# A megakernel of attention, experts and state space: the order of work at the end of the first attention and around the expert gates

## The chip, the cores and the metric

The kernel runs on one NeuronCore of a Trainium2 chip. The metric is the device time of one launch in microseconds (us); the value before is the median of 3 runs. The engines are PE (TensorE: matmuls, with PEld its weight loads), DVE (VectorE), ACT (ScalarE), POOL (GpSimd) and SP (SyncE, which here issues DMAs). The profile is that of one further execution.

## The reference, cut to what matters

Four residual blocks act on `x` (4 batches x 512 rows x 256 channels); `ctx_768` is a context of 1601 rows x 192 channels for each batch. The change lies in the end of the first block and the start of the second and third.

```python
x = x + _L0_xattn_ref(_layernorm(x), ctx_768, ...)      # 16 heads of 16, 1601 keys
x = x + _L0_ffn_ref(_layernorm(x), Wg, W11, W12, W2)    # 8 experts, 2 for each row
x = x + _L1_xattn_ref(_layernorm(x), ctx_768, ...)      # top-32 attention, S4, FFN
x = x + _L1_ffn_ref(_layernorm(x), ...)                 # attention with switched heads

# first block
attn = einsum('bhqd,bhkd->bhqk', q, k) * scale
attn = softmax(clip(attn, -1e4, 1e4))
out = einsum('bhqk,bhkd->bqhd', attn, v) @ Wo + bo
# second block
topk_scores, topk_idx = top_k(softmax(x @ Wg), 2)       # the gates
fused = silu(x @ W11[e]) * (x @ W12[e]);  out = sum of topk_scores * (fused @ W2[e])
# third block
scores = (x @ Wq) . (ctx @ Wk);  only the 32 largest of 1601 are kept, then softmax
```

## The kernel before, in words

**The first attention** is `attend` (L81). Its 16 heads go in groups of four, so with 4 batches there are 16 groups (`gi`, 0 to 15). A head has 32 rows of a tile: 16 of data, one that carries the negated row maximum or the ones for the sum, the rest zero. Four heads of a group therefore stand in four row groups of the PE array and can be multiplied side by side. Per group there are two passes over the 1601 keys. The maxima (`maxima_mm`, L190, PSUM tiles `pss` of pool `ps_s`, three buffers) are scores of 128 queries by 512 keys, which DVE reduces to row maxima `mx`. The weights (`weights_mm`, L229, PSUM tiles `pst` of pool `ps_t`, three buffers) are scores the other way round, 128 keys by 512 queries with the maximum already subtracted, and ACT makes `pT` of them by Exp (L237). `gather` (L240) multiplies `pT` of a chunk of 128 keys with the values of the four heads into the one accumulator `acc`.

The order of PE is written out by hand (`tc.manual_schedule` for PE alone; the other engines are ordered by the framework). A step `t` is half a chunk: two heads of the weights and, 30 steps ahead (`LEAD`), two heads of the maxima of a later group, interleaved. A group has 13 chunks, so `NU` = 26 steps, and there are 416 steps, followed by 40 in which only what is left is emptied. In the last 30 steps there are no maxima left. The gather of a chunk stands four steps behind its weights. Further work (projections of coming groups, and what `at(t, ...)` orders for a later step) is a list of generators, `todo` and `due`, from which `step()` (L299) takes one piece in each odd step, and one more in each step behind the 416th.

When a group's last chunk is gathered, `taken` (L249) copies `acc` to `ou`, sends the sums of the softmax through a DMA (`sums`) to 128 partitions, takes reciprocals and sends them back by a second DMA (`r4`). Eleven steps later `scaled` (L259) spreads them by a matmul (`bc`, L265), and DVE multiplies (`oN`). When all four groups of a batch are there, `output` (L269) multiplies `oN` with `wo` for each of the four tiles of 128 queries (four matmuls each, tile `po` in pool `ps_p`, which has one buffer) and DVE adds the result to the residual `xr` (L277).

Behind the loop (L356 to L367) DVE and one matmul `pn` check that no score was clamped and that all sums are sound, and write `flag`. All engines load `flag` (L720) and branch on it (L721); with the data here the branch is not taken into `attend_any`.

**The second part** (from L734) holds the experts and the second attention. PE, DVE and ACT keep the order of the program there; POOL and SP are ordered by the framework. SP loads the weights of the second attention, the mask `tmask` and the context of batch 0 (`load_ctx2`, L793), and then the gate's weights `wg` (L1017). `run(keys2(0, 0))` (L1256) computes the keys of the second attention for the first two heads of batch 0 (L839, L840, four blocks of up to 512 keys, evicted by ACT, L843, then two mask rows by POOL, L846). Then, for each batch in turn (L1258 to L1267), DVE takes statistics of four tiles (`ln_stats`, L664 to L667, with a power by POOL, L669), normalises (L675), SP writes `xn` to DRAM (`xs`), PE transposes (L773), ACT copies (L774), and 16 small matmuls give the gates `pg` (L1266). The two PSUM buffers of keys and transposes are `mm0` and `mm1` (`bank`, L754). DVE then chooses two experts for each row (L1275 to L1303), PE counts rows by expert (`pc`, L1308), the keys of the other two heads follow on PE (`run(keys2(0, 1))`, L1310), and DVE and PE work out which rows go to which block of 128 (`pt`, L1379; `x_at`, L1383). POOL fetches experts' weights (`wb`) and rows (`xg`) by indirect DMAs (L1399), and PE begins the experts with transposing `xg` (L1422).

The lines that set when the last attention steps and the gates come:

```python
        ps_s = st.enter_context(tc.tile_pool(name="a_s", bufs=3, space=PSUM))
        ps_t = st.enter_context(tc.tile_pool(name="a_t", bufs=3, space=PSUM))
...
                x, y = weights_mm(gi, c, pair, pTs[gi, c]), s_unit(t + LEAD)
                for _ in range(2):
                    next(x), next(y, None)
```

Of the kernel before, what the change touches and what calls it, by code (L numbers as in the profile page):

```python
# [11 lines left out]
F32 = mybir.dt.float32  # L12
# [7 lines left out]
P = 128  # L20
# [60 lines left out]
def attend(nc, tc, a, xr, ident, ones, evac, normalized, flag):  # L81
# [10 lines left out]
    with ExitStack() as st:  # L92
# [135 lines left out]

        def weights_mm(gi, c, pair, pT):  # L229
            wd = P if c < NG - 1 else GL  # L230
            for j in (2 * pair, 2 * pair + 1):
                rows = slice(32 * j, 32 * j + 32)
                pst = ps_t.tile([P, S], F32, name="pst", tag="pst")
                nc.tensor.matmul(  # L234
                    pst[:wd, :], kTs[gi][rows, c * P : c * P + wd], qms[gi][rows, :], start=True, stop=True
                )
                nc.scalar.activation(pT[:wd, j, :], pst[:wd, :], AF.Exp)  # L237
                yield
# [30 lines left out]
        def output(b, qt):  # L269
            po = ps_p.tile([P, C], F32, name="po", tag="pj")  # L270
            for g in range(AG):
                nc.tensor.matmul(
                    po, oNs[b][:, g, qt * P : (qt + 1) * P], w["wo"][:, g, :], start=(g == 0), stop=(g == AG - 1)
                )
# [3 lines left out]
            yield  # L278

        def s_unit(s):  # L280
            gi, i = divmod(s, NU)
            return maxima_mm(gi, i // 2, 1 - i % 2) if gi < B * AG else iter(())
# [33 lines left out]
        for t in range(n_steps + 40):  # L316
# [6 lines left out]
            if gi < B * AG:  # L323
                if pair == 0:
                    pTs[gi, c] = p3.tile([P, 4, S], F32, name="pT", tag="pT")
                x, y = weights_mm(gi, c, pair, pTs[gi, c]), s_unit(t + LEAD)
                for _ in range(2):
                    next(x), next(y, None)
# [25 lines left out]

        m, low, one = [p3.tile([P, B * AG * 16], F32, name=n, tag="pT") for n in ("m", "low", "one")]
        nc.vector.tensor_reduce(m, mx.rearrange("p g q j n -> p (g q j) n"), AX.X, ALU.max)
        nc.vector.tensor_scalar(low, m, CLAMP, None, ALU.is_le)
        cnt = p1.tile([P, 2], F32, name="cnt")  # L360
        nc.vector.scalar_tensor_tensor(low, m, 104.0 - CLAMP, low, ALU.is_ge, ALU.mult, accum_out=cnt[:, 0:1])
        nc.vector.tensor_scalar(one, sums.rearrange("p g c -> p (g c)"), 0.5, None, ALU.is_ge)
        nc.vector.tensor_reduce(cnt[:, 1:2], one, AX.X, ALU.add)
        pn = ps_p.tile([P, 2], F32, name="pn", tag="pj")
        nc.tensor.matmul(pn, ones, cnt, start=True, stop=True)
        nc.vector.tensor_reduce(cnt[:, 0:1], pn, AX.X, ALU.add)
        nc.vector.tensor_scalar(flag, cnt[0:1, 0:1], 2.0 * P * B * AG * 16 - 0.5, None, ALU.is_lt)  # L367
# [255 lines left out]
def kernel(ctx: ExitStack, tc: tile.TileContext, a: dict, out: bass.AP):  # L623
# [114 lines left out]
    with ExitStack() as st:  # L738
# [37 lines left out]


# [13 lines left out]
        ts(tm4, tmask, 1.0 / XH, None, ALU.mult)  # L791
# [224 lines left out]
        wg = p_s.tile([P, 2, FE], F32, name="wg")  # L1016
        nc.sync.dma_start(wg, a["f_wg"].rearrange("(k p) e -> p k e", p=P))  # L1017
# [3 lines left out]
        nc.vector.tensor_copy(step, step_i)  # L1021
# [234 lines left out]
        run(keys2(0, 0))  # L1256
        pg = ps_b.tile([P, NT, FE], F32, name="pg", tag="po", bufs=1)
        for b in range(B):  # L1258
            xn = p_s.tile([P, QT, C], F32, name="xn", tag="s4", bufs=NSB)
            normalize([xn[:, i, :] for i in range(QT)], [xr[b * QT + i] for i in range(QT)])  # L1260
            nc.sync.dma_start(xs[b * S : (b + 1) * S, :].rearrange("(i p) c -> p i c", p=P), xn)
            xnT = p_s.tile([P, 2, S], F32, name="xnT", tag="s4", bufs=NSB)
            run(channels(xnT, [xn[:, i, :] for i in range(QT)]))
            for i in range(QT):
                for k in range(2):
                    nc.tensor.matmul(  # L1266
                        pg[:, b * QT + i, :], xnT[:, k, i * P : (i + 1) * P], wg[:, k, :], start=(k == 0), stop=(k == 1)  # L1267
                    )
        sm = p_s.tile([P, NT, FE], F32, name="sm")
# [8 lines left out]
        nc.scalar.activation(sm, sm, AF.Exp)  # L1278
        nc.vector.tensor_reduce(gm, sm, AX.X, ALU.add)
# [30 lines left out]
        run(keys2(0, 1))  # L1310
# [859 lines left out]
```

## Time and profile before

| | |
|---|---|
| median of 3 runs | 3650.86 us (3633.21 to 3656.53) |
| the profiled execution | 3655.28 us, its span 3653.5 us |
| mean granted clock of PE | 0.890 |
| busy: PE, DVE, ACT, POOL | 84%, 64%, 44%, 25% of the span |
| last maxima of the first attention | about 1031 us |
| last gather of the first attention ends | 1090.9 us |
| flag written | 1115.2 us |
| first instruction behind the branch | 1119.7 us |
| gates done, DVE begins to choose | 1165.5 us |
| `x_at` written | 1200.3 us |
| first matmul of the experts | 1203.6 us |

Times of day are from the span's start. Shares of busy time are averages over all stages; the stretch from 1031 to 1204 us is read from the timeline, where each line has start, length, engine, line of the program, operation and tiles, and in brackets the idle time before it and what ended it. An fp32 matmul is recorded as two passes, so `x8` is four matmuls.

### The profile page before, as it was taken

To read this page: it belongs to the slowest core of one execution; us is meant where nothing else is said; L and a number is where in the kernel's file an instruction comes from. 1 tells how busy PE (TensorE), PEld (TensorE's weight loads), DVE (VectorE), ACT (ScalarE), POOL (GpSimd) and SP (SyncE) were. 2 spreads that over 40 slices of the span, in tenths; PEclk is the share of its full clock that TensorE was granted. 3 is DMA by queue.
4 is the path that set the end of the run, shared out by engine and by line. 5 is a ranking of instruction groups with operands and counts; after the bars stand their busy time and mean duration, and the time that the engine had idled before them with its cause. 6 is when DMAs were issued, how large, how long until landed. Compare 5 with 4: busy or idle time off the path is not lost. (4 is left out here: it accounts for less than half of the span.)

```text
span 3653.5 us, 41683 instructions
## 1 busy us (share of the span) xinstructions
PE 3073.6 (84%) x16046; PEld 1704.0 (47%) x16046; DVE 2330.0 (64%) x3959; ACT 1619.5 (44%) x3326; POOL 930.9 (25%) x603
## 2 busy tenths in 40 slices
PE   6999999999986599789787977599865788887898
PEld 3433333333324599456555555466632334344354
DVE  3665565656623699598999899333326674766754
ACT  0254454445550377355555555122232344453454
POOL 1000000000001377410010100033317392763935
PEclk8699999999995699788898888799977798888899
DMA  2000000000001488300000000200010000000000
GB/s 68 1 15 1 1 15 1 1 1 1 1 1 51 132 291 281 117 28 14 1 14 1 1 1 1 96 1 0 1 38 0 0 1 5 2 2 5 1 6 6
DMA packets 48913, 110.03 MB, mean 30 GB/s; under 512 B 10450, under 2 KB 26139, under 8 KB 48700
## 3 DMA queue, kind: packets, MB, share of 16 engines
q0 software_dynamic: 20256, 70.66, 5.9%
q1 hardware_dynamic: 28444, 36.55, 3.2%
q8 instruction: 131, 2.15, 0.2%
q14 instruction: 82, 0.67, 0.1%
HBM read 97.62 MB, written 9.31 MB: 29 GB/s over the span
## 5 line engine op out<-in xcount | busy, mean ns | idle before, releaser
L203 DVE TENSOR_REDUCE mx<-pss 128x1 f32<-128x512 f32 x768 | 494.3, 685 | 294.2 <-PE pss L199 290.8
L237 ACT ACTIVATE pT<-pst 128x512 f32<-128x512 f32 (+1 forms) x832 | 452.5, 594 | 507.2 <-PE pss L199 318.8
L234 PE MATMUL pst<-qm,kT 32*128 32x512 f32 (+1 forms) x1664 | 507.0, 639 | 8.0 <-ACT pT L237 8.0
L199 PE MATMUL pss<-kT,qT 32*128 32x512 f32 x1536 | 485.7, 678 | 1.5 <-DVE mx L203 1.5
L981 PE MATMUL sum<-dg,e 128*128 128x128 f32 (+1 forms) x1664 | 267.6, 324 | 118.8 <-ACT dg L957 118.7
L1982 POOL TENSOR_TENSOR agg<-agg,tmp 128x1024 f32<-128x1024 f32 x112 | 263.3, 2378 | 336.0 <-DVE tmp L1981 335.8
L1933 ACT ACTIVATE pe<-pss,dnm 128x512 f32<-128x512 f32 x256 | 173.8, 683 | 337.8 <-DVE dnm L1931 337.6
L981 PEld LDWEIGHTS sum<-dg,e 128*128 128x128 f32 (+1 forms) x1664 | 239.2, 226 | 176.5 <-ACT dg L957 138.8
L1931 DVE TENSOR_REDUCE dnm<-pss 128x1 f32<-128x512 f32 x256 | 164.6, 684 | 196.3 <-PE pss L1928 195.9
L234 PEld LDWEIGHTS pst<-qm,kT 32*128 32x128 f32 (+1 forms) x1664 | 146.2, 180 | 294.6 <-ACT pT L237 270.7
L1873 POOL TENSOR_TENSOR dv<-dv,tmp 128x1024 f32<-128x1024 f32 x112 | 263.4, 2352 | 53.8 <-PE pss L1928 46.1
L1928 PE MATMUL pss<-dkT,dqT 64*128 64x512 f32 x512 | 182.9, 702 | 83.9 <-ACT pe L1933 83.2
L244 PE MATMUL acc<-pT,v 128*32 128x512 f32 (+1 forms) x1664 | 221.8, 604 | 0.0
L1872 DVE TENSOR_TENSOR tmp<-pp,mix 128x1024 f32<-128x1024 f32 x112 | 136.2, 1222 | 62.7 <-POOL dv L1873 49.1
L1431 PE MATMUL pa<-xgT,wb 128*128 128x128 f32 x1248 | 159.0, 282 | 19.6 <-ACT xgT L1424 19.5
L1399 POOL DMA_INDIRECT wb<-in_f_w,w_at x117 | 141.1, 1206 | 120.5 <-DVE t L1359 29.1
L199 PEld LDWEIGHTS pss<-kT,qT 32*128 32x128 f32 x1536 | 148.8, 193 | 36.2 <-DVE mx L203 24.8
L1431 PEld LDWEIGHTS pa<-xgT,wb 128*128 128x128 f32 x1248 | 154.0, 198 | 23.3 <-ACT xgT L1424 20.0
L1942 ACT COPY dpT<-tp 128x512 f32<-128x512 f32 x256 | 138.1, 595 | 53.9 <-PE tp L1940 53.5
L1940 PEld LDWEIGHTS tp<-ident,pe 128*128 128x128 f32 x1024 | 124.8, 148 | 60.7 <-issue 34.7
L931 DVE MAX8 tops<-ones 128x8 f32<-128x401 f32 x256 | 147.0, 574 | 6.7
L890 PE MATMUL pss<-xkT,xqT 64*128 64x512 f32 (+1 forms) x512 | 148.8, 610 | 2.7 <-ACT sc L897 1.3
(408 smaller groups left out, 5529.4 us busy)
## 6 DMA issues: line engine op xcount, KB each, us to landing
c<-in_ctxT SPq DMA_DIRECT2D x8, 800.5 KB
ys<-yo SPq DMA_DIRECT2D x39, 128.0 KB
c<-in_ctxT SPq DMA_DIRECT2D x8, 400.2 KB
xr<-in_x SPq DMA_DIRECT2D x16, 128.0 KB
xs<-xn SPq DMA_DIRECT2D x4, 512.0 KB
fwd<-in_dft SPq DMA_DIRECT2D x1, 2048.0 KB
inv<-in_idft SPq DMA_DIRECT2D x1, 2048.0 KB
out_dram<-ot SPq DMA_DIRECT2D x16, 128.0 KB
```

What stands on the lines that cost most here:

```text
L199: nc.tensor.matmul(pss[:, :wd], qTs[gi][rows, qt * P : (qt + 1) * P], kTs[gi][rows, o : o + wd], start=True, stop=True,)
L203: nc.vector.tensor_reduce(mx[:, gi, qt, j, n : n + 1], pss[:, :wd], AX.X, ALU.max)
L234: nc.tensor.matmul(pst[:wd, :], kTs[gi][rows, c * P : c * P + wd], qms[gi][rows, :], start=True, stop=True)
L237: nc.scalar.activation(pT[:wd, j, :], pst[:wd, :], AF.Exp)
L244: nc.tensor.matmul(acc[32 * j : 32 * j + 32, :], vs[b][:wd, c, AG * g + j, :], pT[:wd, j, :], start=(c == 0), stop=(c == NG - 1), tile_pos ...
L981: nc.tensor.matmul(pm[:w, c - 4 * n, :], e[:, c * P : c * P + w], dg, start=(h == 0 and c == 4 * n), stop=(h == 3 and c == cols[-1]),)
L1431: nc.tensor.matmul(pa[:, c, :], wbs[i, half][:, o : o + P], xTs[i][:, k, :], start=(k == 0), stop=(k == 1))
L1873: nc.gpsimd.tensor_tensor(v_t, v_t, tmp, ALU.add)
L1928: nc.tensor.matmul(pss[j], qT[rows, it * P : (it + 1) * P], kT[rows, :], start=True, stop=True)
L1931: nc.vector.tensor_reduce(nm, pss[j], AX.X, ALU.max, negate=True)
L1933: nc.scalar.activation(pe, pss[j], AF.Exp, bias=nm, accum_out=sums[u][:, it, j : j + 1])
L1982: nc.gpsimd.tensor_tensor(aggs[b][it], aggs[b][it], tmp2, ALU.add)
```

## The change

It has four pieces.

1. In steps without maxima (`lone`), all four heads' weights of a chunk are issued in the even step (`x` and a second generator `y` for the other two heads), and none in the odd step. Their PSUM tiles alternate between `ps_s`, which the maxima no longer use, and `ps_t`.
2. The outputs of the last batch are no longer one `output` for each query tile. `output_most` multiplies the first three groups 12 steps behind group 14's last gather, into two PSUM tiles `po2` of `ps_s` that stay open, each for two query tiles; `output_rest` adds the fourth group behind `scaled(15)`, and DVE adds to `xr`.
3. The check that writes `flag` becomes the generator `checked`, ordered 10 steps behind the last gather, ahead of `scaled(15)` in PE's order.
4. In the second part, `wg` is loaded first and kept in pool `p1`; the gates of the batches come ahead of any keys and are staggered: statistics of batch b, then normalising and transposing of batch b - 1, then the gate matmuls of batch b - 2. Converting `step`, `row`, `before`, `token` and `tm4` on DVE moves behind that loop. Of `keys2(0, 0)` one block is issued behind the gates' Exp; its other three blocks and `keys2(0, 1)` follow behind `pc`.

```diff
--- before.py
+++ after.py
@@ -226,11 +226,17 @@
             nc.vector.tensor_tensor(qms[gi], tp.rearrange("p a b -> p (a b)"), qTs[gi], ALU.add)
             yield
 
+        lone, last = [False], [0]
+
         def weights_mm(gi, c, pair, pT):
             wd = P if c < NG - 1 else GL
             for j in (2 * pair, 2 * pair + 1):
                 rows = slice(32 * j, 32 * j + 32)
-                pst = ps_t.tile([P, S], F32, name="pst", tag="pst")
+                last[0] ^= 1
+                if lone[0] and last[0]:
+                    pst = ps_s.tile([P, S], F32, name="pst", tag="pss")
+                else:
+                    pst = ps_t.tile([P, S], F32, name="pst", tag="pst")
                 nc.tensor.matmul(
                     pst[:wd, :], kTs[gi][rows, c * P : c * P + wd], qms[gi][rows, :], start=True, stop=True
                 )
@@ -275,6 +281,51 @@
                 if g == 1:
                     yield
             nc.vector.tensor_tensor(xr[b * QT + qt], po, xr[b * QT + qt], ALU.add)
+            yield
+
+
+        pos = []
+
+        def output_most(qt):
+            b = B - 1
+            if qt % 2 == 0:
+                pos.append(ps_s.tile([P, 2, C], F32, name="po2", tag="pss"))
+            for g in range(AG - 1):
+
+                nc.tensor.matmul(
+                    pos[-1][:, qt % 2, :], oNs[b][:, g, qt * P : (qt + 1) * P], w["wo"][:, g, :],
+                    start=(g == 0 and qt % 2 == 0), stop=False,
+                )
+                if g == 0:
+                    yield
+            yield
+
+        def output_rest(half):
+            b, g = B - 1, AG - 1
+            for i in range(2):
+                q = slice((2 * half + i) * P, (2 * half + i + 1) * P)
+                nc.tensor.matmul(
+                    pos[half][:, i, :], oNs[b][:, g, q], w["wo"][:, g, :], start=False, stop=(i == 1)
+                )
+            for i in range(2):
+                x = xr[b * QT + 2 * half + i]
+                nc.vector.tensor_tensor(x, pos[half][:, i, :], x, ALU.add)
+            yield
+
+        def checked():
+
+
...
+            pn = ps_p.tile([P, 2], F32, name="pn", tag="pj")
+            nc.tensor.matmul(pn, ones, cnt, start=True, stop=True)
+            nc.vector.tensor_reduce(cnt[:, 0:1], pn, AX.X, ALU.add)
+            nc.vector.tensor_scalar(flag, cnt[0:1, 0:1], 2.0 * P * B * AG * 16 - 0.5, None, ALU.is_lt)
             yield
 
         def s_unit(s):
@@ -324,8 +375,13 @@
                 if pair == 0:
                     pTs[gi, c] = p3.tile([P, 4, S], F32, name="pT", tag="pT")
                 x, y = weights_mm(gi, c, pair, pTs[gi, c]), s_unit(t + LEAD)
+                lone[0] = t + LEAD >= n_steps
+                if lone[0]:
+
+                    y = weights_mm(gi, c, 1, pTs[gi, c])
                 for _ in range(2):
-                    next(x), next(y, None)
+                    if not lone[0] or pair == 0:
+                        next(x), next(y, None)
             s = t + LEAD + 1
             if s % NU == 0 and s // NU <= B * AG:
                 done = s // NU - 1
@@ -340,8 +396,14 @@
                     gather(g2, i2 // 2, pTs.pop((g2, i2 // 2)))
                     if i2 // 2 == NG - 1:
                         taken(g2)
+                        if g2 + 1 == B * AG:
+                            at(t + 10, checked())
                         at(t + 11, scaled(g2))
-                        if g2 % AG == AG - 1:
+                        if g2 + 2 == B * AG:
+                            at(t + 12, (None for qt in range(QT) for _ in output_most(qt)))
+                        if g2 + 1 == B * AG:
+                            at(t + 14, (None for half in range(2) for _ in output_rest(half)))
+                        elif g2 % AG == AG - 1:
                             for qt in range(QT):
                                 at(t + 13 + 2 * qt, output(g2 // AG, qt))
             if pair == 1:
@@ -351,20 +413,6 @@
             if gi >= B * AG:
                 step()
         assert not todo and not late and not due and not now
-
-
-
...
-        nc.vector.tensor_scalar(flag, cnt[0:1, 0:1], 2.0 * P * B * AG * 16 - 0.5, None, ALU.is_lt)
 
 
 def attend_any(nc, tc, a, xr, ident, ones, evac, normalized, to_channels):
@@ -774,6 +822,8 @@
                 then(lambda k=k, tp=tp: nc.scalar.copy(dst[:, k, :], tp.rearrange("p a b -> p (a b)")))
                 yield
 
+        wg = p1.tile([P, 2, FE], F32, name="wg")
+        nc.sync.dma_start(wg, a["f_wg"].rearrange("(k p) e -> p k e", p=P))
 
         wq = p1.tile([P, 2, 2, P], F32, name="xwq")
         nc.sync.dma_start(wq, a["x_wq"].rearrange("(k p) (c m) -> p k c m", p=P, c=2))
@@ -788,7 +838,6 @@
         tmask = p1.tile([P, NT], U8, name="tmask")
         nc.sync.dma_start(tmask, a["tmask"])
         tm4 = p1.tile([P, NT], F32, name="tm4")
-        ts(tm4, tmask, 1.0 / XH, None, ALU.mult)
         cs, kTs, vs, qTs = {}, {}, {}, {}
 
         def load_ctx2(b):
@@ -1013,20 +1062,14 @@
         ys = dram.tile([NBK * P, C], F32, name="ys")
         NSB = 10
 
-        wg = p_s.tile([P, 2, FE], F32, name="wg")
-        nc.sync.dma_start(wg, a["f_wg"].rearrange("(k p) e -> p k e", p=P))
         step_i = p_s.tile([P, P], I32, name="step_i")
         nc.gpsimd.iota(step_i, pattern=[[1, P]], base=0, channel_multiplier=0)
         step = p_s.tile([P, P], F32, name="step")
-        nc.vector.tensor_copy(step, step_i)
         row_i = p_s.tile([P, 1], I32, name="row_i")
         nc.gpsimd.iota(row_i, pattern=[[0, 1]], base=0, channel_multiplier=1)
         row = p_s.tile([P, 1], F32, name="row")
-        nc.vector.tensor_copy(row, row_i)
         before = p_s.tile([P, P], F32, name="before")
-        ts(before, step, row, None, ALU.is_gt)
         token = p_s.tile([P, NT], F32, name="token")
-        ts(token, step[:, 0:NT], float(P), row, ALU.mult, ALU.add)
 
         u = da = ph = quarter = angle0 = fmax = fmin = None
 
@@ -1253,19 +1296,37 @@
 
 
         setup = s4_setup()
-        run(keys2(0, 0))
         pg = ps_b.tile([P, NT, FE], F32, name="pg", tag="po", bufs=1)
-        for b in range(B):
-            xn = p_s.tile([P, QT, C], F32, name="xn", tag="s4", bufs=NSB)
-            normalize([xn[:, i, :] for i in range(QT)], [xr[b * QT + i] for i in range(QT)])
+        xns, xnTs, mvs = {}, {}, {}
+
+        def normal(b):
+            xn = xns[b] = p_s.tile([P, QT, C], F32, name="xn", tag="s4", bufs=NSB)
+            mv, rs = mvs.pop(b)
+            for i in range(QT):
+                ts(xn[:, i, :], xr[b * QT + i], mv[:, i, 0:1], rs[:, i : i + 1], ALU.subtract, ALU.mult)
             nc.sync.dma_start(xs[b * S : (b + 1) * S, :].rearrange("(i p) c -> p i c", p=P), xn)
-            xnT = p_s.tile([P, 2, S], F32, name="xnT", tag="s4", bufs=NSB)
-            run(channels(xnT, [xn[:, i, :] for i in range(QT)]))
+
+        def gated(b):
             for i in range(QT):
                 for k in range(2):
                     nc.tensor.matmul(
-                        pg[:, b * QT + i, :], xnT[:, k, i * P : (i + 1) * P], wg[:, k, :], start=(k == 0), stop=(k == 1)
+                        pg[:, b * QT + i, :], xnTs[b][:, k, i * P : (i + 1) * P], wg[:, k, :], start=(k == 0), stop=(k == 1)
                     )
+
+        for b in range(B + 2):
+            if b < B:
+                mvs[b] = ln_stats([xr[b * QT + i] for i in range(QT)])
+            if 0 < b <= B:
+                normal(b - 1)
+                xnTs[b - 1] = p_s.tile([P, 2, S], F32, name="xnT", tag="s4", bufs=NSB)
+                run(channels(xnTs[b - 1], [xns[b - 1][:, i, :] for i in range(QT)]))
+            if b > 1:
+                gated(b - 2)
+        nc.vector.tensor_copy(step, step_i)
+        nc.vector.tensor_copy(row, row_i)
+        ts(before, step, row, None, ALU.is_gt)
+        ts(token, step[:, 0:NT], float(P), row, ALU.mult, ALU.add)
+        ts(tm4, tmask, 1.0 / XH, None, ALU.mult)
         sm = p_s.tile([P, NT, FE], F32, name="sm")
         gm = p_s.tile([P, NT], F32, name="gm")
 
@@ -1276,6 +1337,8 @@
         nc.vector.tensor_reduce(gm, sm, AX.X, ALU.max)
         tt(sm, sm, wide(gm), ALU.subtract)
         nc.scalar.activation(sm, sm, AF.Exp)
+        first_keys = keys2(0, 0)
+        next(first_keys)
         nc.vector.tensor_reduce(gm, sm, AX.X, ALU.add)
         nc.vector.reciprocal(gm, gm)
         tt(sm, sm, wide(gm), ALU.mult)
@@ -1307,7 +1370,7 @@
         flat = both.rearrange("p t e -> p (t e)")
         nc.tensor.matmul(pc[:, 0, :, :].rearrange("p t e -> p (t e)"), before, flat, start=True, stop=True)
         nc.tensor.matmul(pc[:, 1, :, :].rearrange("p t e -> p (t e)"), ones, flat, start=True, stop=True)
-        run(keys2(0, 1))
+        run(first_keys, keys2(0, 1))
         s0, s1 = [p_s.tile([P, NT, FE], F32, name=n) for n in ("s0", "s1")]
         nc.vector.tensor_copy(s0, pc[:, 1, :, :])
         place = p_s.tile([P, NT, FE], F32, name="place")
```

More of the change, by code (lines that the diff above doesn't have):

```diff
@@ L278, in output @@
             yield
+        pos = []
[23 more added lines that the diff above has]
+        def checked():
+            m, low, one = [p3.tile([P, B * AG * 16], F32, name=n, tag="pT") for n in ("m", "low", "one")]
+            nc.vector.tensor_reduce(m, mx.rearrange("p g q j n -> p (g q j) n"), AX.X, ALU.max)
+            nc.vector.tensor_scalar(low, m, CLAMP, None, ALU.is_le)
+            cnt = p1.tile([P, 2], F32, name="cnt")
+            nc.vector.scalar_tensor_tensor(low, m, 104.0 - CLAMP, low, ALU.is_ge, ALU.mult, accum_out=cnt[:, 0:1])
+            nc.vector.tensor_scalar(one, sums.rearrange("p g c -> p (g c)"), 0.5, None, ALU.is_ge)
+            nc.vector.tensor_reduce(cnt[:, 1:2], one, AX.X, ALU.add)
+            pn = ps_p.tile([P, 2], F32, name="pn", tag="pj")
[3 more added lines that the diff above has]
+            yield
         def s_unit(s):
@@ L353, in attend @@
         assert not todo and not late and not due and not now
[L357 to L367, printed above, removed]
 def attend_any(nc, tc, a, xr, ident, ones, evac, normalized, to_channels):
```

## The prediction

> **What bounds the kernel now.** I read the page's slices first, then the timeline of the stretch that the diff touches, then the waits of each engine in it, then windows for the granted clock. The chain of waits does not help: its pieces begin at 2317.80 us, behind the last branch, so the stretch must be read from the timeline.
>
> Slices of 91.3 us: busy tenths of PE and the granted clock.
> ```profile
> PE   6999999999986599789787977599865788887898
> PEclk8699999999995699788898888799977798888899
> ```
> The thirteenth slice (1096 to 1187 us) is the hole: PE busy six tenths at half clock. It holds the end of the first attention and the routing, which is what the diff edits.
>
> The last 15 chunks of the first attention, from about 1031 us, have no maxima beside them. One chunk (start, length, engine, line):
> ```profile
> 1074.04 1.12 PE L234 MATMUL pst<-qm,kT 32*128 32x512 f32 x2 [0.67 <-ACT pT L237]
> 1075.09 1.06 PE L244 MATMUL acc<-pT,v 128*32 128x512 f32 x8
> 1076.09 1.13 PE L234 MATMUL pst<-qm,kT 32*128 32x512 f32 x6
> 1077.24 1.57 ACT L237 ACTIVATE pT<-pst 128x512 f32<-128x512 f32 x3 [1.45 <-PE pst L234]
> 1077.89 1.12 PE L234 MATMUL pst<-qm,kT 32*128 32x512 f32 x2 [0.67 <-ACT pT L237]
> ```
> Each fp32 matmul is two passes, so x6 is three heads, side by side in 1.13 us, because a head uses 32 rows of the array. There are three pst buffers. The fourth head waits 0.67 us for ACT and then runs alone for 1.05. A chunk takes 3.85 us (1074.04 to 1077.89). Four at once is seen in the main loop, where pst and pss share the row groups:
> ```profile
> 1002.00 0.69 PE L234 MATMUL pst<-qm,kT 32*128 32x512 f32 x1
> 1002.01 0.69 PE L199 MATMUL pss<-kT,qT 32*128 32x512 f32 x1
> 1002.02 0.69 PE L234 MATMUL pst<-qm,kT 32*128 32x512 f32 x1
> 1002.02 0.69 PE L199 MATMUL pss<-kT,qT 32*128 32x512 f32 x1
> 1003.16 1.57 ACT L237 ACTIVATE pT<-pst 128x512 f32<-128x512 f32 x3 [1.59 <-PE pss L199]
> ```
> The tail, in order, and the branch that reads the flag:
> ```profile
> 1096.10 2.04 PE L265 MATMUL bc<-r,spread 4*128 4x512 f32 x2 [5.22 <-DMA r<-rs]
> 1098.99 3.78 PE L272 MATMUL po<-wo,oN 128*128 128x256 f32 x8 [0.85 <-DVE oN L266]
> 1115.01 0.14 DVE L367 TENSOR_SCALAR flag<-cnt 1x1 int32<-1x1 f32 x1
> 1119.70 0.23 POOL L1019 IOTA step_i<- 128x128 int32 x1 [485.88 <-DVEq L721]
> ```
> The engines' branch behind the flag, from the view of its line (length in ns, start):
> ```profile
> L721 PEldq COMPARE_BRANCH  x1: 3448/3448/3448, 1115.8 to 1115.8; - x1
> ```
> The sums go through DMA twice (PE idle 5.2 us, and its clock falls), four output tiles follow, then the flag, then PE's branch of 3.45 us; all engines leave together near 1119.7. Then the second part:
> ```profile
> 1125.61 0.17 DVE L791 TENSOR_SCALAR tm<-tmask 128x16 f32<-128x16 uint8 x1 [10.46 <-DMA mrow<-in_vmask]
> 1129.52 2.05 PE L839 MATMUL pk<-c,xwk 128*128 128x512 f32 x2 [14.74 <-DMA c<-in_ctxT]
> 1165.49 0.29 DVE L1275 COPY sm<-pg 128x128 f32<-128x128 f32 x1 [11.78 <-PE pg L1266]
> 1176.78 1.13 PE L839 MATMUL pk<-c,xwk 128*128 128x512 f32 x2
> ```
> The same in a window (busy time of PE, PEld, DVE, ACT, POOL; then granted clock, DMA share, GB/s):
> ```profile
> 1130.00:1166.00 36.00, 34.48 (x112) 23.80 (x110) 12.48 (x45) 6.66 (x12) 6.08 (x5) 0.50 0.17 59
> ```
> DVE stands behind tmask, and PE behind the context (14.7 us) for keys that nothing needs yet; the gates come behind both, and PE runs all of it at clock 0.50, a 128x512 matmul in 2.05 us a pair of passes against 1.13 at 1176.78.
>
> **The change, part by part** (positive is saved).
>
> *A, chunks of four heads.* Removed per chunk: the wait of 0.67 and the lone head's 1.05. Left on PE: four heads at once, 1.05 from start to the gather's start (1077.89 to 1078.94), and the gather, 1.00 to the next heads (1075.09 to 1076.09): 2.05. ACT needs 4 x 0.485 = 1.94 (three take 1.57, one 0.60, so one more costs 0.485), so PE and ACT are nearly even. The fourth head's second buffer use frees when ACT has done two heads of the chunk before: 1.16 + 0.60 + 0.485 + 0.05 = 2.30 after that chunk's start; the period settles between, at 2.175. From the gather at 1032.80 to that at 1086.60 there are 14 periods, 53.8 us; they become 14 x 2.175 = 30.5. Added: 0.5 at the start, where buffers of the last maxima are still read (1031.19 to 1032.13); 0.65 for the transposes of the last row maxima, 1.05 for group 14's bc, 0.6 for the copy of acc, all of which hid in the old waits; seven of the twelve early output matmuls, 0.5 each (1111.88: four in 1.99 us), less 0.6 taken up by the slack: 2.9; and 1.6 in the last chunk, because the second po2 leaves only one ps_s buffer. So 30.5 + 7.3 = 37.8, a gain of 16.0. Behind it come five more output matmuls and the last gathers: 1.0 + 1.0 + 1.05 + 0.5 + 1.0 + 1.1 = 5.65, where 1086.60 to 1090.88 is 4.28: 1.4 lost. A = 14.6. Bounds: 0 (a period of 3.4) and 20 (2.05, outputs free); I take the one near the main loop's four at once.
>
> *B, tail.* From acc's end E (1090.88) the two DMAs, bc and oN stay: oN at E + 8.05. The first three groups' output matmuls are gone from here; four matmuls are left at half clock, 0.95 each (3.78 for four): E + 11.9; the last two additions (0.42 each, 0.45 apart) end at E + 12.85. The check's DVE work (1.22, 0.29, 0.42, 0.23, 0.42) and its matmul fit into the DMA waits, being covered by the 5.2 us; if that cover were gone it would cost about 1 us, for pn stands ahead of bc on PE. The flag is written at about E + 4.3. PE's load of the flag (0.49) and its branch (3.45) can then run while DVE still adds: E + 8.2 + 0.4 + 0.49 + 3.45 = E + 12.5, with DVE's own load last, E + 13.5. Before, it was 1119.70 - 1090.88 = 28.8. B = 15.3. Bounds: 12.7 (the branch waits for the last matmul, E + 11.9 + 4.2) and 17 (full clock: bc 1.13, oN at E + 7.15, the branch at E + 11.6).
>
> *C, gates first.* From the common start X: DVE needs no DMA. Statistics of a batch take 2.42 (1126.36 to 1128.78), POOL's power is covered by the next batch's statistics, normalising takes 1.38: the second batch is normal at X + 10.1. Then PE is unbroken: rest of its transposes to X + 11.1, four gates of 3.6 (16 matmuls, 1150.17 to 1154.03 less a wait of 0.26) and two more transpositions of 1.75: X + 29.0. ACT's copies (0.59 x 2) hide, as gates run two batches behind. The old time is 1165.45 - 1119.70 = 45.75. C = 16.7. wg's DMA, moved past nine on SP's queue, is issued in 0.41 and is not waited for; it puts the context 0.45 later, and no one waits for that now. Converting step, row, tmask (1.1 us of DVE) now hides behind PE's gates. Bounds: 14 (DVE and PE not overlapped so well) and 24 (clock rises, rival 2).
>
> *D, keys behind the routing.* One block runs on PE during the 6.9 us in which DVE chooses experts: free. The other three stand ahead of the second half's four, behind pc. From pc's start (1172.39) the old keys end at +9.4 and PE then waits until +13.1 for rows. New: in full-clock time 2.1 + 2.1 + 0.87 + 7.2 = 12.3; if the clock rises after 3.4 us, as at 1176.78, they end at +15; wholly at half clock, at +23.5. With the first, pt begins 1.9 late, but its matmuls run in half of 7.05, and x_at is no later than rows of the second half allow, about +25 against +27.9. POOL takes that back: the mask rows (3.1 to 3.4 us a pair) of the first half now fall among the six weight fetches (1.28 each), which end about +25, and xg queues behind their bytes. D = 0. Bounds: -10 (pt starts at +23.5 and takes 7.05 twice: +37.6) and +4.
>
> **Sum.** 14.6 + 15.3 + 16.7 + 0 = 46.6. The profiled execution took 3655.3 (span 3653.5): 3608.7. It is 4.4 over the median of the three runs, so on the median's scale 3604.
>
> **Rivals.**
> 1. *Keys become the bound* (D at its bad end): the row for it is 1129.52 to 1142, keys at half clock for 13 us. Then 3604 + 10 = 3614. Against it: the keys behind pc did speed up.
> 2. *The clock rises in the gates.* For it: outputs sped up at about 1111 us after 12 us of work. Against: the window 1130 to 1166 stays at 0.50 with PE busy 34.5 of 36. Then PE's 18 us behind X + 11 take about 11: 3597. The Trainium skill (TensorE: Matmul & The Clock Gate, Part 1) says the clock is raised after one busy window, about 3.4 us; by that rule this rival would be the forecast. The trace of before disagrees in that window. By the rule the sum is 3597, by the row 3604.
> 3. *The chunks only come down to 2.9 to 3.3 us*, for want of free buffers or because PE cannot pass from four row groups to the gather without draining. The additions then partly hide, some 5 us of them left: A = 53.8 - 14 x period - 5 - 1.4, 1 to 7, and 3612 to 3617. Against it: the main loop makes the same passage from eight heads to the gather with no idle time of its own.
> 4. *Given back in the experts*: weights, not xg, start them. Half of C goes and D is at its bad end: 3604 + 8 + 10 = 3622.
> 5. *Slower: heads one by one.* If the three ps_s buffers came free only in turn with ACT, each head would take 1.13 + 0.62, a chunk 7.0 + 1.0 = 8.0 and A = 14.6 - 14 x (8.0 - 2.175) = -67; B and C give 32, and the time is 3651 + 35 = 3686. It decides from a chunk of 2.175 + 46.6/14 = 5.5 us on. Against it: with six buffers two heads at least are free at once.
>
> **How the numbers follow.** Forecast 0.46, rival 1 0.14, rival 2 0.15, rival 3 0.14, rival 4 0.06, rival 5 0.05. About 1%, 36.5 us, is what a measurement here can tell from no change, so the border is 3614. Faster: 0.43 + 0.15 and half of rivals 1 and 3, 0.14: 0.72. Slower: 0.02, the rest 0.26. The range takes rival 2 with the runs' own spread (17 under the median) below, and rivals 1, 3 and 4 above: 3580 to 3626. The likeliest alone: 3594 to 3614.
>
> **What would show it.** A: gathers 2.2 us apart from 1035 us on and ACT's 1.45 us idle gone. B: the first POOL iota about 13.5 us behind acc's last gather, with the flag written before bc. C: no PE wait for the context, sm's copy 29 us behind that iota. D: xg's first transpose near +31 behind pc. The prediction is wrong if the gathers stay over 3 us apart, if the branch begins only behind the last addition, or if pt waits for the keys by more than 5 us.

## The result, and the profile after

| | before | after |
|---|---|---|
| median of 20 runs (us) | 3655.31 | 3625.27 |
| lowest to highest | 3633.21 to 3687.92 | 3610.92 to 3638.82 |
| profiled execution; its span | 3655.28; 3653.5 | 3634.1; 3632.2 |

The ratio is 0.9918, with an interval of 0.9899 to 0.9938: 30.0 us saved (22.7 to 36.9), or 0.8%. 3625 lies inside the range by 0.7 us, at its upper edge, and outside the likeliest case's own.

For the readings below, the stretch is cut at six marks: M, the last row maximum; E, acc's end (the start of its copy); X, the first instruction behind the branch; S, the copy of the gates; pc, the places' matmul; XG, the first transpose of the experts' rows.

| stage (us) | before | after | saved | forecast |
|---|---|---|---|---|
| M to E (A) | 58.75 | 43.96 | 14.8 | 14.6 |
| E to X (B) | 28.78 | 15.87 | 12.9 | 15.3 |
| X to S (C) | 45.79 | 27.88 | 17.9 | 16.7 |
| S to pc | 6.90 | 6.89 | 0 | 0 |
| pc to XG (D) | 31.23 | 41.58 | -10.4 | 0 |
| M to XG | 171.45 | 136.18 | 35.3 | 46.6 |

The 35.3 lies inside the interval of the medians. The two profiled executions differ by less, 21.3: after's stood 4.7 us later already at M (1036.89 against 1032.17), ahead of all changed code, and lost 9.3 behind XG. Most of the 9.3 is in the last stage, whose code is the same, where one execution ran a stretch at half clock and the other did not. The same pair of matmuls, first after, then before, from the timeline of PE:
```profile
2686.44 3.78 PE L1951 MATMUL pk<-dxT,d_wk 128*128 128x512 f32 x4 [0.69 <-ACT dqT L1947]
```
```profile
2713.29 1.98 PE L1888 MATMUL pk<-dxT,d_wk 128*128 128x512 f32 x4 [0.69 <-ACT dqT L1884]
```
It need not all be chance. From XG to the end the changed kernel took 2459.1 here and 2459.0 when profiled again (e8, below), against 2449.9 before and 2453.9 and 2452.3 in e1 and e2, which keep the old second part; and the medians save 30.0 where the stages up to XG save 35.3. On the other hand e5, which has the gates first too, took 2453.9. Whether the change costs some 5 us there, or only the clock does, no run settles.

After, the slices (90.8 us each):
```profile
PE   6999999999997699688887877699764787887898
PEclk6799999999995899888989888899867798888899
```
The thirteenth slice (1090 to 1180 us) still holds the hole: PE is busy seven tenths there instead of six, at a clock of still five tenths.

*A.* The timeline of the lone chunks: start, length, engine, line, then what the engine had waited for.
```profile
1048.20 1.14 PE L240 MATMUL pst<-qm,kT 32*128 32x512 f32 x8
1049.27 1.07 PE L250 MATMUL acc<-pT,v 128*32 128x512 f32 x8
1049.42 4.07 ACT L243 ACTIVATE pT<-pst 128x512 f32<-128x512 f32 x8 [0.29 <-PE pst L240]
1050.27 1.41 PE L240 MATMUL pst<-qm,kT 32*128 32x512 f32 x8
1051.61 1.07 PE L250 MATMUL acc<-pT,v 128*32 128x512 f32 x8
...
1061.65 1.06 PE L250 MATMUL acc<-pT,v 128*32 128x512 f32 x8
1062.64 1.13 PE L295 MATMUL po<-wo,oN 128*128 128x256 f32 x4
1063.70 1.14 PE L240 MATMUL pst<-qm,kT 32*128 32x512 f32 x8
```
Heads are x8, four of two passes, in 1.14; gathers with nothing else between them start by turns about 2.07 and 2.33 apart (2.34 in the pair above), 2.2 in the mean, where 2.175 was forecast. ACT's idle time ahead of a group is 0.29, where it was 1.45. Two output matmuls (x4) stand between two chunks and cost their full 1.06.

*B.* The same view, at the tail's end, and the branch by line (length in ns, start):
```profile
1085.11 0.14 DVE L328 TENSOR_SCALAR flag<-cnt 1x1 int32<-1x1 f32 x1
...
1088.90 3.78 PE L307 MATMUL po<-wo,oN 128*128 128x256 f32 x8 [0.85 <-DVE oN L272]
1092.72 0.76 DVE L312 TENSOR_TENSOR xr<-po,xr 128x256 f32<-128x256 f32 x2 [0.95 <-PE po L307]
1096.65 0.43 DVE L712 BATCH_NORM_STATS2 ln_st<-xr 128x6 f32<-128x256 f32 x1 [3.17 <-DVEq L769]
1096.72 0.23 POOL L1066 IOTA step_i<- 128x128 int32 x1 [459.82 <-DVEq L769]
```
```profile
L769 PEldq COMPARE_BRANCH  x1: 3522/3522/3522, 1089.5 to 1089.5; - x1
L769 PEldq EVENT_SEMAPHORE  x1: 51/51/51, 1093.1 to 1093.1; - x1
L769 DVEq COMPARE_BRANCH  x1: 72/72/72, 1093.4 to 1093.4; - x1
L769 DVEq EVENT_SEMAPHORE  x1: 21/21/21, 1096.5 to 1096.5; - x1
```
PE is behind its branch at 1093.1, beside the additions, as forecast. DVE branches only behind its last addition, and 3.1 us pass until its event: its record of 72 ns does not show them, the gap to the event does. The profile of before has such a gap of 3.7 us, in the view of which the prediction showed PE's line alone:
```profile
L721 DVEq COMPARE_BRANCH  x1: 72/72/72, 1115.8 to 1115.8; - x1
L721 DVEq EVENT_SEMAPHORE  x1: 21/21/21, 1119.5 to 1119.5; - x1
```

*C and D.* Windows of after: busy PE, PEld, DVE, ACT, POOL; granted clock, DMA share, GB/s. First X to S, then pc to the routing's pt, then pt to x_at.
```profile
1096.72:1124.60 27.88, 21.11 (x97) 20.04 (x98) 14.76 (x58) 4.68 (x8) 5.68 (x14) 0.50 0.54 168
1131.49:1155.96 24.47, 23.67 (x33) 7.89 (x33) 20.11 (x59) 3.14 (x6) 7.73 (x5) 0.50 0.19 64
1155.96:1169.87 13.91, 13.87 (x65) 13.72 (x64) 0.00 (x1) 0.21 (x1) 4.97 (x4) 0.50 0.27 77
```
The two last, before:
```profile
1172.39:1185.50 13.11, 9.40 (x20) 3.60 (x20) 10.84 (x47) 1.98 (x4) 1.22 (x1) 0.76 0.12 40
1185.50:1200.33 14.83, 14.10 (x64) 13.81 (x64) 8.62 (x14) 0.00 (x0) 8.79 (x7) 0.50 0.58 176
```
From pc to pt it takes 24.47 us at clock 0.50, with PE busy 23.67 of them; the seven blocks of keys fill 22.5 of that (1133.48 to 1155.96). The rows for pt's first half are written early enough: DVE begins them at pc + 11.84, as before. So pt, once it starts, runs without a break, but 11.4 us later than before (24.47 against 13.11):
```profile
1143.33 5.00 DVE L1437 TENSOR_TENSOR rows<-step,slot 128x1024 f32<-128x1024 f32 x2
1151.73 2.35 DVE L1437 TENSOR_TENSOR rows<-step,slot 128x1024 f32<-128x1024 f32 x2
1155.96 13.87 PE L1442 MATMUL pt<-ids,rows 128*128 128x39 f32 x64
1169.87 0.20 DVE L1446 CAST x_at<-pt 128x39 int32<-128x39 f32 x1 [15.79 <-PE pt L1442]
```

### The profile page after: what moved, and what is told of

It reads as the page before. It is cut to its first block, busy times and chain, and to the rows that moved or that the text cites. A ratio compares the mean times of both kernels' runs of the same rounds, so it can differ in the third digit from the quotient of the medians.

```text
span 3632.2 us, 41689 instructions
## 1 busy us (share of the span) xinstructions
PE 3063.2 (84%) x16046; PEld 1699.6 (47%) x16046; DVE 2330.0 (64%) x3959; ACT 1615.9 (44%) x3326; POOL 930.9 (26%) x603
## 5 line engine op out<-in xcount | busy, mean ns | idle before, releaser
L240 PE MATMUL pst<-qm,kT 32*128 32x512 f32 (+1 forms) x1664 | 494.9, 642 | 0.7 <-ACT pT L243 0.7
L199 PEld LDWEIGHTS pss<-kT,qT 32*128 32x128 f32 x1536 | 149.3, 194 | 35.8 <-DVE mx L203 24.8
L1494 PEld LDWEIGHTS pa<-xgT,wb 128*128 128x128 f32 x1248 | 152.8, 197 | 24.5 <-ACT xgT L1487 20.5
L1991 PEld LDWEIGHTS pss<-dkT,dqT 64*128 64x128 f32 x512 | 56.3, 201 | 202.0 <-ACT pe L1996 146.6
```

Source lines behind the costliest of these rows:

```text
L199: nc.tensor.matmul(pss[:, :wd], qTs[gi][rows, qt * P : (qt + 1) * P], kTs[gi][rows, o : o + wd], start=True, stop=True,)
L240: nc.tensor.matmul(pst[:wd, :], kTs[gi][rows, c * P : c * P + wd], qms[gi][rows, :], start=True, stop=True)
L1494: nc.tensor.matmul(pa[:, c, :], wbs[i, half][:, o : o + P], xTs[i][:, k, :], start=(k == 0), stop=(k == 1))
L1991: nc.tensor.matmul(pss[j], qT[rows, it * P : (it + 1) * P], kT[rows, :], start=True, stop=True)
```

## The experiments

Three questions: what each part does alone, what D's loss hangs on, and what B's last 2.4 us are. Ratios are to runs of the kernel before on the same chip.

**e1_lone: the chunks of four heads alone** (before with piece 1 of the change; shown is where the heads are issued).
```diff
+                lone[0] = t + LEAD >= n_steps
+                if lone[0]:
+                    y = weights_mm(gi, c, 1, pTs[gi, c])
                 for _ in range(2):
-                    next(x), next(y, None)
+                    if not lone[0] or pair == 0:
+                        next(x), next(y, None)
```


> Before plus piece 1 alone (four heads at a time). Theory (the parts add up as the stage times of the two traces say): gathers 2.2 us apart; from the gather two steps ahead of the first lone chunk to the end of acc 61.9 us before, about 41 here, because nothing but the last row maxima, one bc and the copy of acc is added; tail and gates as before. Gain about 20 us, ratio 0.9945. Rival (the early outputs are what fills PE, and the chunks by themselves are bound by ACT and its buffers near 3 us): gain 9 to 12.

Measured: 0.9928 (0.9893 to 0.9963). M to E and pc to pt:
```profile
1041.55:1077.50 35.95, 35.58 (x258) 9.63 (x254) 3.57 (x7) 31.18 (x62) 0.00 (x0) 1.00 0.01 1
1155.55:1169.63 14.08, 14.08 (x20) 4.82 (x20) 11.81 (x47) 1.76 (x3) 1.22 (x1) 0.50 0.11 37
```
PE is busy 35.58 of 35.95: chunks alone save 22.8 of 58.75, more than the 20.5 forecast, and the tail behind E is 3.5 shorter (25.29) without an edit there: three of its four output tiles ran at the higher clock (2.0 us instead of 3.78), where before only one did. So of the change's 43.96, 8.0 are the early outputs. The second line is unexpected: with the old order of keys, four blocks behind pc run at 0.50, where before's profile has 0.76. In e2 they do so too.

**e2_tail: the outputs and the check moved, heads as before, second part as before** (shown against after; the lines of piece 4 are taken back too).
```diff
-                lone[0] = t + LEAD >= n_steps
+                lone[0] = False
```


> Before plus pieces 2 and 3 alone (early outputs, flag ahead of bc), chunks of two and two as before. Theory: the twelve early matmuls (6 us) go mostly into PE's waits of 0.67 us a chunk and of the emptying steps, so acc ends 0 to 3 us later, and from there to the first instruction behind the branch it takes 16.0 instead of 28.8: gain 10 to 13 us, ratio 0.997. Rival (PE works in order, so the waits for ACT stay as they are and the matmuls come on top): acc ends 6 us later, gain 7.

Measured: 0.9952 (0.9918 to 0.9986). E to X is 15.59, so the tail's gain (13.2) needs no other part. M to E grew by 7.6, but the clock fell in that window:
```profile
1030.16:1096.51 66.35, 61.60 (x284) 17.05 (x282) 3.80 (x8) 33.18 (x63) 0.00 (x0) 0.92 0.00 1
```
e3 shows 4.5 of growth there at the same clock with unchanged code, so about 3.1 belong to the outputs. That the rest of them hides in the old chunks' waits for ACT is argued from these lengths, not tried alone. In the new chunks they do not hide: outputs and last chunk cost 8.0, where the prediction's price was 5.9.

**e3_gates: gates first and keys behind the routing, the first attention as before** (piece 4 whole; shown are its lines on the keys).
```diff
-        run(keys2(0, 0))
...
+        first_keys = keys2(0, 0)
+        next(first_keys)
...
-        run(keys2(0, 1))
+        run(first_keys, keys2(0, 1))
```


> Before plus piece 4 alone (gates ahead of the keys). Theory: from the first instruction behind the branch to the copy of the gates 27.9 us instead of 45.8 (saves 17.9), and seven blocks of keys at half clock ahead of pt cost 10.4: gain 7.5 us, ratio 0.998. If the clock rises in the keys, about 16 to 20. Rival (the cost behind pc came from the early fetches of the shortened tail, not from the keys): pt is not late here and the gain is 17.

Measured: 1.0002 (0.9973 to 1.0031). X to S is 27.88, 17.9 saved; pc to XG is 41.60, 10.4 lost. The rest, 7.5 us or 0.2%, is too small to be seen in the time. Windows of M to E, of a piece of it, and of pc to pt:
```profile
1036.24:1099.51 63.27, 55.26 (x260) 13.03 (x258) 3.80 (x8) 33.18 (x63) 0.00 (x0) 0.92 0.00 1
1050.00:1064.00 14.00, 11.98 (x44) 2.77 (x40) 0.25 (x1) 6.22 (x12) 0.00 (x0) 0.69 0.01 1
1163.14:1187.60 24.46, 23.66 (x32) 7.88 (x32) 20.11 (x59) 3.15 (x6) 7.73 (x5) 0.50 0.20 64
```
The code of the first two is before's: 0.69 for 14 us is a dip of the clock, and the window is 4.5 us longer than before's. The third repeats after's 24.47 to 0.01 us.

The parts by stages, M to XG: e1 24.8, e2 4.8, e3 3.0; e2 and e3 without their dips 9.3 and 7.5. Their 41.6 exceed the whole's 35.3 because the outputs lose their cover (8.0 less 3.1, 4.9) and the 3.5 that e1's tail gained from the clock cannot be gained beside e2's; against that, e1 and e2 paid some 1.5 each for the half clock behind pc, which is in D already. That makes 36.2; 0.7 of what is left is e2's gain from X to S.

**e8_changed_again: the changed kernel once more.**

> The changed kernel as it is, beside the others on one chip. Theory: the same stages as in its first profile (44.0 us from the last row maximum to the copy of acc, 15.9 to the first instruction behind the branch, 27.9 to the copy of the gates, 38.4 from pc to x_at), ratio to before 0.990 to 0.993; what differs elsewhere, some 5 us at a time, is the clock. Rival (the keys' half clock behind pc was chance in the first profile): pt starts 13 to 15 us behind pc.

Measured: 0.989 (0.9849 to 0.9931). All stages up to XG repeat within 0.2 us (M to E 43.95, pc to XG 41.54) and so does the clock behind pc:
```profile
1134.52:1158.99 24.47, 23.67 (x32) 7.89 (x33) 20.12 (x59) 3.15 (x6) 7.75 (x5) 0.50 0.19 64
```

**e4_keys_late: the seven blocks behind the experts.**
```diff
-        run(first_keys, keys2(0, 1))
...
         run(powers)
+        run(first_keys, keys2(0, 1))
```


> The changed kernel, with all keys of batch 0 but the first block moved behind the experts, into the stretch of 32 us in which PE waits for the experts' rows. Theory: pt waits for DVE's rows alone, x_at comes 27 us or less behind pc instead of 38.4, and the first expert with it: 10 to 11 us less than the changed kernel, about 3614 in median, ratio to before 0.9888. Rival A (x_at is not what starts the experts; POOL's weight fetches and their bytes are): xg's transpose comes at most 4 us earlier. Rival B (the keys late delay the second attention's first scores by what they take, 12 to 22 us): no gain or a loss against the changed kernel.

Measured: 0.9895 (0.9852 to 0.9938). pc to pt, and pt to x_at:
```profile
1131.41:1144.62 13.21, 1.20 (x5) 0.94 (x5) 10.93 (x47) 0.00 (x0) 3.56 (x3) 0.50 0.14 44
1144.62:1158.50 13.88, 13.84 (x64) 13.69 (x64) 6.45 (x13) 0.00 (x0) 3.56 (x4) 0.50 0.52 186
```
Without keys pt starts at pc + 13.21 and XG comes at + 30.42 instead of + 41.58: the keys on PE cost 11.2 us, and no weights fetch holds the experts back. The same seven blocks take 12.0 us behind the experts, at clock 1.00 (1452.60 to 1464.58), so it is the half clock that made them long behind pc. M to XG is now 46.8 under before; that the prediction's sum was 46.6 is chance: B saves 2.1 less than forecast in e4, and A, C and D 2.2 more. But from the experts' last matmul to the first scores it takes 40.97 instead of 33.55. On POOL's queue the mask rows stand between the fetches of the experts' results:
```profile
1461.38 3.21 POOL L895 TENSOR_SCALAR xkT<-mrow 1x1601 f32<-1x1601 uint8 x2 [2.05 <-DMA yg<-ys,y_at]
...
1474.77 3.39 POOL L895 TENSOR_SCALAR xkT<-mrow 1x1601 f32<-1x1601 uint8 x2 [1.99 <-DMA yg<-ys,y_at]
```
Two pairs, 6.6 us, with some 2 us of idle time ahead of each, and the stretch is 7.4 longer.

**e5_keys_split, e10_keys_split_again: three blocks behind pc, four behind the experts** (the same kernel twice).
```diff
-        run(first_keys, keys2(0, 1))
+        run(first_keys)
...
         run(powers)
+        run(keys2(0, 1))
```


> The changed kernel, with the three remaining blocks of the first half's keys left behind pc and only the second half's four moved behind the experts. Theory: three blocks take 9.3 us at half clock and end before DVE has rows (12 to 13 us behind pc), so they are free: x_at as with all keys moved, 27 to 28 us behind pc, 10 us less than the changed kernel. Rival (any keys there cost, by POOL's mask rows of 3 to 4 us ahead of the weight fetches and beside DVE's rows, which took 5.0 instead of 2.35 us): x_at 30 us or more behind pc, only half of the 10 us.

Measured, e5: 0.9882 (0.9839 to 0.9925). From pc to pt:
```profile
1126.17:1140.61 14.44, 10.48 (x17) 3.90 (x17) 12.17 (x47) 1.39 (x3) 2.67 (x2) 0.50 0.00 0
```
The wait for rows covers three blocks at half clock: pt at + 14.44, XG at + 31.81. That is 1.2 and 1.4 later than in e4; the first of DVE's instructions on the rows takes 2.54 us beside POOL's mask rows, and 1.22 in e4, so this part of the rival holds. One pair of mask rows is left behind the experts, and that stretch is 38.05, 4.5 longer than after's.

> The same kernel as the one with the second half's keys directly behind the experts, beside the other on one chip. Theory: 4.6 us slower than it, ratio to before 0.988. Rival: equal within 2 us.

Measured, e10: 0.9868 (0.9834 to 0.9901); XG at + 31.77, the stretch behind the experts 38.92. By stages the split is some 5 us better than the change (9.8 less 4.5 to 5.4); its intervals and the change's overlap, so the time alone does not separate them. It has the lowest ratio of the versions run here. Beside e9 (below) it was expected 4.6 us slower; its median is 13 us lower (3616.3 against 3629.5).

**e6_no_adds: the change without the last four additions** (the last batch's attention is not added to its residual).
```diff
-            for i in range(2):
-                x = xr[b * QT + 2 * half + i]
-                nc.vector.tensor_tensor(x, pos[half][:, i, :], x, ALU.add)
```


> The changed kernel without the four additions of the last batch's attention to its residual (that part of the sum is left out). Theory (DVE's own way through the branch is last: its last addition, 0.6 us of loading the flag, then 3.1 us between its branch and its next event): DVE gets there 3.8 us earlier, PE's branch of 3.5 us becomes last, and from the end of acc to the first instruction behind the branch it takes 12.6 instead of 16.0 us. Rival (a fixed cost of 3.2 us of the join behind whichever engine is last): DVE was not the cause, PE's branch ends at the same time as before, and it stays at 16.0.

Measured: 3630.2 in one execution; E to X 12.69 instead of 15.87. The branch by line:
```profile
L766 DVEq COMPARE_BRANCH  x1: 72/72/72, 1093.2 to 1093.2; - x1
L766 PEldq COMPARE_BRANCH  x1: 3722/3722/3722, 1093.9 to 1093.9; - x1
L766 DVEq EVENT_SEMAPHORE  x1: 21/21/21, 1096.1 to 1096.1; - x1
L766 PEldq EVENT_SEMAPHORE  x1: 51/51/51, 1097.7 to 1097.7; - x1
```
With nothing to add, DVE is behind its branch at 1096.1 and PE's is last. So in the change DVE's branch, 3.1 us behind the last addition, sets X, and PE's is some 3 us from being the bound itself.

**e7_keys_in_experts: four blocks spread over the experts' loop, the other three as in e5.**
```diff
+        more_keys = keys2(0, 1)
...
+            if i >= 8 and i % 4 == 0:
+                next(more_keys, None)
         run(powers)
-        run(keys2(0, 1))
+        run(more_keys)
```


> The changed kernel with three blocks of the first half's keys behind pc and the second half's four blocks one by one into the loop of the experts (behind its iterations 8, 12, 16 and 20). Theory: what the late keys gave back came from POOL's two mask rows (3.2 us a pair) among its fetches of the experts' results; in the loop they hide, so the experts' rows to the first scores take 33 us again instead of 38.0, xg comes 31.8 us behind pc, and the loop grows by at most the four blocks' 7.2 us of PE, less its idle time: 4 us or less. Against the changed kernel 6 to 10 us saved, 3615 to 3619 where that one has 3625, ratio to before 0.989. Rival (PE bounds the experts): the loop grows by all 7 us and nothing is won against keys behind the experts.

Measured: 0.9911 (0.9887 to 0.9936), so the 6 to 10 us were not saved: its median is 10 us above that of e8, the changed kernel beside it. The stretch behind the experts is 33.60 again, but the experts' loop grew from e5's 289.15 to 306.59. Each as one window, e5 first:
```profile
1157.98:1447.13 289.15, 250.49 (x2207) 232.79 (x2207) 245.21 (x350) 195.11 (x491) 177.91 (x148) 0.93 0.73 237
```
```profile
1163.03:1469.62 306.59, 259.75 (x2223) 235.75 (x2223) 247.60 (x350) 196.67 (x495) 177.19 (x150) 0.93 0.68 224
```
PE has 9.3 us more to do, and its waits in the window show 7.6 new ones (3.2 ahead of po with no releaser shown, 2.2 for a copy by ACT, 2.2 for weights): 16.9 of 17.4. PE was idle for 38.7 of e5's 289.15, but the four blocks did not go into that idle time. Why, and why the three waits follow, was not tried.

**e9_keys_beside_top: those four blocks behind the first scores.**
```diff
         run(powers)
-        run(keys2(0, 1))
...
+        run(fours(0))
+        for _ in keys2(0, 1):
+            release()
         pair = scores2(2)
...
-            if n == 0:
-                run(fours(0))
```


> The changed kernel with three blocks of the first half's keys behind pc, and the second half's four issued behind the first half's scores of the second attention, where DVE has two heads' selection to do (about 13 us each) before it needs them. Theory: xg comes 31.8 us behind pc, and from the experts' last output to the first scores it takes 33 us again, as POOL's mask rows no longer stand ahead of the first rows of the experts; the four blocks, 7 us at full clock, hide beside DVE. About 10 us less than the changed kernel, ratio to before 0.987. Rival (the rest of the second attention pays: DVE waits for scores or for rows fetched late behind the mask rows): from the first scores to the end it takes 5 us or more longer, and nothing is won against the keys directly behind the experts.

Measured: 0.9891 (0.9861 to 0.9921). The edit also moves `fours(0)` ahead of the second scores. The first scores come 32.48 behind the experts, but from there to the end it takes 2147.0, where e10, beside it on the same chip, took 2134.2 and no other run here over 2139.7. The waits in the stretch (total, times, longest, in us):
```profile
PE pss L939 <- POOL xkT L895: 6.1, 1, 6.1
...
POOL yg L1462 <- DVE xr L1549: 29.4, 4, 12.4
```
PE waits for mask rows, which stand on POOL's queue behind fetches that wait for DVE. What `fours(0)` adds to the loss was not tried alone. So each of the later places gives some of it back: e4 and e5 behind the experts, e7 in their loop, e9 behind the scores.

## Why the prediction was right and where it was wrong

**D failed, and it decides.** The sentence "if the clock rises after 3.4 us, as at 1176.78, they end at +15; wholly at half clock, at +23.5. With the first, pt begins 1.9 late" took the wrong branch: the keys ran wholly at half clock, to + 24.5, pt took 13.9, and x_at came at + 38.4, where the bad bound said + 37.6. Rival 1 came true, at -10.4 for its -10, and so did the prediction's own last sign of being wrong: pt waits for the keys, and starts 11.4 us later, where more than 5 was the sign. The row it was taken from was real but no rule: the clock of 0.76 behind pc is seen in one profiled execution, that of before, while e1 and e2, with the same four blocks there, show 0.50, and after, e3, e6 and e8 show 0.50 and pt at + 24.5 with the seven. e4 settles the mechanism: without the keys, 11.2 us return. A row seen once, where the clock is in play, bore the whole term; the half clock of 1129 to 1142, in the same profile, is what every other execution shows behind pc.

**B, 15.3 forecast, 12.9 measured.** "With DVE's own load last, E + 13.5" named the right engine, but charged only its load. DVE's branch takes 3.1 us more until it goes on, 1093.4 to 1096.5. The order of the rest was right: the flag was written at E + 4.3, PE branched beside the additions, and e6's 12.69 is what the stage takes with PE last. The price of DVE's branch stood in the view of before, unread.

**A, 14.6 forecast, 14.8 measured,** through two errors that nearly cancel: chunks gave 22.8 (e1) for 20.5, and the outputs and the last chunk cost 8.0 for 5.9. Rivals 3 and 5 fell: the period is 2.19, and PE passes from four row groups to the gather without idle time.

**C, 16.7 forecast, 17.9 measured.** The order of events was right; the four batches' gates took 3.3 to 3.4 us each for the 3.6 charged. Rival 2 fell. In 1106 to 1128 of after PE is busy without a break, and the clock stays at half:
```profile
1106.00:1128.00 22.00, 22.00 (x92) 19.10 (x91) 8.89 (x34) 3.82 (x7) 1.74 (x2) 0.50 0.39 126
1134.00:1168.00 34.00, 34.00 (x85) 18.53 (x83) 18.91 (x53) 3.35 (x7) 12.70 (x9) 0.50 0.25 78
```
The Trainium skill (TensorE: Matmul & The Clock Gate, Part 1) has the clock raised after about 3.4 us of sustained work. Both windows disagree, six and ten times that long, with matmuls of 8 to 512 columns alike; in e1's tail the clock did rise after one output tile of 3.78 us. What keeps it at half here stays open.

**Rival 4 fell:** the experts' loop and the stretch from there to the first scores take 290.93 and 33.55 after, 289.88 and 32.82 before; D's bad end, which it shares with rival 1, did come.

**The sum.** 10.4 in D and 2.4 in B lost, 0.2 in A and 1.2 in C gained: 46.6 - 11.4 = 35.2, to rounding the table's 35.3. By that sum the forecast of 3604 becomes 3615. Of the 10 us from there to 3625, 4.5 come from the median of before, which is 3655.3 over 20 runs and was 3650.9 over three, and 5.3 are what the medians save less than the stages do. So that the time falls inside the range, by 0.7 us, is in good part luck: the range was made wide for rivals 1, 3 and 4, and the likeliest case did not happen. The chance of 0.72 on faster by over 1% rested on D being free; with D at its bad end the sum lies on the border, and the measured saving of 0.8% is under it.

## What to carry to other kernels

Work that is moved "behind" a stage must be priced at the slowest clock that the trace shows for such work near that place; a faster row counts only once several executions show it. Ask of every new place which queue the moved work's small companions join: here some 3 us of mask rows on POOL, and not the matmuls, undid much of the places behind the experts and behind the scores. And where a flag decides a branch, each engine pays its own branch behind its own last instruction; the engine with the latest work sets the start.

## What the runs showed of the hardware

- The branch costs each engine its own amount, from the branch to the event behind it (after): PE 3.6 us, DVE 3.1, ACT 2.7 (1085.8 to 1088.5), POOL and SP 0.5 and less. It is not fixed: in before, where PE, DVE and ACT branch within 0.1 us of each other, it is 3.5, 3.7 and 3.7.
- Two instructions of DVE on step and slot (two inputs of 128x1024) took 5.00 us beside POOL's mask rows (4.07), and 2.35 alone (in after's second half, and in e4, which has no mask rows there), where POOL's took 3.12. The Trainium skill (GPSIMD Engine Reference, Specifications) says that GpSimd's access to SBUF is shared with VectorE and contends where a VectorE instruction reads two inputs from SBUF; the trace agrees.
- The clock differs between executions of the same code: 1.00 and 0.92 from M to E in before and e3, 4.5 us, and M itself, ahead of every change, lay between 1030.2 and 1041.6 us. A stage's own length at the same granted clock, not its place in the span, can be compared.
